# Order of gate products, routing parts, turned inputs and scatters in a gated cross-attention with a mixture of experts

## Chip, core and metric

The kernel runs on one core of a Trainium2 chip. The metric is the device time in microseconds of one execution. A profiled execution adds a trace, from which the views below are taken; its span runs from the first to the last instruction.

## What is computed

All tensors are float32. x is 32 x 112 x 256, the context 32 x 375 x 256.

```python
x = x + tanh(g_xattn) * xattn(ctx, layernorm(x))     # 16 heads of 64
x = x + tanh(g_ffn) * ffn(layernorm(x))

def xattn(ctx, lat):                 # per batch element
    kv = concat([ln_m(ctx), ln_l(lat)])      # 487 keys
    q, (k, v) = ln_l(lat) @ Wq, split(kv @ Wkv)
    return softmax(q @ k.T / 8) @ v @ Wout
def ffn(x):                          # 3584 tokens, 8 experts, the best 2
    s = softmax(x @ gate_w); w, e = top_k(s, 2); w = w / w.sum()
    return sum(w[j] * (gelu(x @ w1[e[j]] + b1[e[j]]) @ w2[e[j]] + b2[e[j]]))
```

## The kernel before

**Attention.** Two batch elements share a group g of eight steps; step n = 8g + m works on four heads of one element, and there are 128 steps (LAST = 128, NG = 4). The engines run in the order in which the Python code issues instructions (a manual schedule): each engine has a queue, and an instruction that waits holds all behind it on its engine. Step n issues, in the loop from L1201: the score matmuls (`scores`, L449) of step n+1, the row maxima on VectorE (L459), the exponentials on ScalarE (L469); then five slots h = 0 to 4. A slot holds products of keys and values on TensorE (lists `slots` and `pe`), then for h < 4 the four transposes of one head's probabilities (`turn_attn`, L490, copied by VectorE at L494, for h = 2 by ScalarE), the division of half the probabilities (`norm`, L481 and L483), small parts left by an earlier slot (`soon_`, on GpSimd), the VectorE parts of the slot (list `dve`), one pending scatter (`outgoing`) and one pending part of the routing (`extra`). At the start of an even step n the output of the two steps before it is formed (`attend`, L504).

**Keys and values.** Each pair of batch elements needs seven products of blocks instead of eight (`seven`). The first and fourth (p1, p5) are copied by ScalarE (L400, L412), p6 and p7 are added to those by VectorE (L404, L408), GpSimd then adds two blocks (L394), and p2, p4, p3 are added by VectorE (L418). In odd steps p1, p6, p7, p5 are of keys and p2, p4, p3 of values; in even steps the other way round. The sums of inputs that these products use are made by GpSimd (`input_sums`, L333) in step m = 4, one per slot.

**PSUM.** All products, transposes and turned inputs share four buffers (tag `m`, pool `ps_m`). As the trace has it, a new tile takes the buffer that was let go first. Scores and expert outputs have two others (`ps_s`).

**Inputs.** A batch element's context and x are normalised (statistics L227 and L228 in m = 6, 7; roots L248 to L257 on GpSimd in the next slot, applied by ScalarE, L261, in m = 0, 2) and turned in m = 1 and m = 3 of the group before their use (`turn`, L291), half k = 0 copied by ScalarE (L299), half k = 1 by VectorE (L303).

**Slabs and gates.** Tokens are handled in 28 slabs of 128; a group g > 0 has up to two finished slabs, u = 0 and u = 1. `project` (L539, m = 0), `residual` (L549 and statistics, with a GpSimd root L559, L561 left in `soon_`), `normed` (L567 on VectorE, then a copy L570 on GpSimd in the next slot) and `logits_of` (a product L577 of 128 x 256 per expert, eight per slab, with a read of 0.08 us) belong to a slab. `normed` and six products are in step m = 2 + 2u, two in each of h = 1 to 3; the last two products come in h = 0 of the step after.

**Routing.** Slabs form routing groups of 4, 4, 4, 4, 4, 4, 2 and 2. In the step of a group's last two products `extra` gets the routing's parts, which are popped one per slot: eight parts of small VectorE and GpSimd work; `counts` (L632 to L635, GpSimd); `places` (two matmuls, L641 of `both` and L642 of `had`, which `counts` makes); `gates` (reads the place tile at L646); for the first group the stranger parts (L698, L710); `slots_of` (L662); `out_to`, which fills `outgoing` with one scatter (L673, an indirect DMA on GpSimd's queue) per slab and choice. Routings begin in steps 27, 45, 61, 83, 99, 117 and 125.

**Towards the experts.** In step 120 `counted` (L752) takes the counts so far, and `locate_early` finds the first six blocks of 128 rows; SP loads them in step 123 (`fetch_rows`, L875) after the scatters issued up to then. `turn_rows(t)` turns the rows of block t (L893) and copies them (L897); `hidden(t)` (L906, L913) and `second(t)` (L919) are the expert's two layers; `combine(t)` scales (L935) and adds into the output by an indirect DMA on GpSimd's queue (L936). Blocks 0 to 2 are begun in steps 125 to 127 and in the tail after the loop, where also the last two slabs are projected, routed on VectorE and scattered, and `locate_late` (L761 to L806) finds the other blocks. Then `run` works through the blocks.

Of the kernel before, what the change touches and what calls it, by code (L numbers as in the profile page):

```python
# [23 lines left out]
def kernel(  # L24
# [20 lines left out]
    nc = tc.nc  # L45

    P = 128
    B, S, D = x.shape
# [38 lines left out]
    NG = NP // 2  # L87
# [78 lines left out]
    if True:  # L166
# [45 lines left out]
        outgoing = []  # L212
# [785 lines left out]
        def do(parts):  # L998
            for part in parts:
                part()  # L1000
# [63 lines left out]
        LAST = B * NG  # L1064
        fills = {1: 3, 2: 3, 3: 2}
        sums_at = {0: (0, 2), 1: (1, 1), 2: (0, 3), 3: (1, 2), 4: (0, 0), 5: (1, 3)}
        filled, extra = 0, []
        for n in range(LAST):
            if n % NG == 0:
                b = n // NG  # L1070
                if b + 4 < B:
                    load(b + 4)
                for _ in range(fills.get(b, 0)):
                    fill(filled)
                    filled += 1
            g, m = divmod(n, 2 * NG)


            jk, jv, odd = (n + 3) // 2, n // 2, n % 2
            for kv, j in ((0, jk), (1, jv)):  # L1080
                if (kv, j) not in ahead and j < LAST // 2:
                    ahead[kv, j], behind[kv, j] = seven(kv, j)
            none = [lambda: None] * 4
            one, two = ((1, jv), (0, jk))[odd], ((0, jk), (1, jv))[odd]
            one, two = ahead.get(one, none), behind.get(two, none)
            if n < LAST - 5:
                slots = [[two[0], one[0]], [two[1]], [one[1], two[2]], [one[2]], [one[3]]]
            else:

                for j in (LAST // 2 - 2, LAST // 2 - 1):  # L1090
                    if (1, j) not in ahead:
                        ahead[1, j], behind[1, j] = seven(1, j)
                (p1, p6, p7, p5), (p2, p4, p3) = ahead[1, LAST // 2 - 2], behind[1, LAST // 2 - 2]
                (q1, q6, q7, q5), (q2, q4, q3) = ahead[1, LAST // 2 - 1], behind[1, LAST // 2 - 1]
                slots = {
                    5: [[two[0], one[0]], [two[1], one[1]], [two[2], p1], [one[2], p6], [one[3]]],
                    4: [[two[0], p7], [two[1], p5], [two[2], p2], [p4, q1], [p3, q6]],
                    3: [[q7], [q5], [q2], [q4], [q3]],
                }.get(LAST - n, [[], [], [], [], []])

            qn = [n] if n < LAST - 8 else {LAST - 8: [n, n + 1], LAST - 7: [n + 1, n + 2, n + 3]}.get(n, [])
            for n_ in qn:
                qg, qi = divmod((n_ + 3) // 2, NG)
                if qg < B // 2:
                    slots[1].insert(0, lambda qg=qg, i=qi + NG * (1 - n_ % 2): q_unit(qg, i))

            pe = [[], [], [], [], []]
            dve = [[], [], [], []]  # L1110
            if n in sums_at:
                dve[1].append(lambda: weight_sums(*sums_at[n]))

            nb = 2 * g + 2
            if nb < B:
                if m in (0, 2):
                    for h in range(4):
                        dve[min(h + 1, 3)].append(then[nb + m // 2][h])
                if m == 1:
                    pe[1] += [lambda: turn(nb, 0), lambda: turn(nb, 1, nc.vector)]  # L1120
                if m == 3:
                    pe[1] += [lambda: turn(nb + 1, 0), lambda: turn(nb + 1, 1, nc.vector)]
                if m == 4:
                    for h, part in enumerate(input_sums(g + 1)):
                        dve[h].append(part)
                if m in (6, 7) and nb + 2 < B or n == 1:
                    u = m - 4 if m > 1 else 1
                    ln_now, then[nb + u] = ln_parts(nb + u)
                    for h in range(4):
                        dve[h].append(ln_now[h])  # L1130
            if n == 1:
                nc.scalar.activation(tg[:, :2], tg[:, :2], AF.Tanh)
                nc.scalar.mul(tg[:, 2:3], tg[:, 1:2], 0.5)
            if n == 3:
                dve[2].append(b1_turned)

            for u in range(2):
                i = ended(2 * g - 2 + u) if g > 0 else None
                if m == 6 + u and ended(2 * g + u) is not None:
                    load_slab(ended(2 * g + u))  # L1140
                if i is None:
                    continue
                if m == 0:
                    pe[2 + 2 * u].append(lambda i=i: project(i))
                if m == u:
                    dve[3 - 3 * u].append(lambda i=i: residual(i))
                if m == 2 + 2 * u:
                    dve[0].append(lambda i=i: normed(i))
                    for h in range(1, 4):
                        dve[h].append(lambda h=h, i=i: logits_of(i, 2 * h - 2, 2 * h))  # L1150
                if m == 3 + 2 * u:
                    dve[0].append(lambda i=i: logits_of(i, 6, 8))
                    if group[i][1] == groups[group[i][0]] - 1:

                        r, (hits, ids, ids_out) = route_parts(group[i][0], nc.gpsimd)
                        extra = [[part] for part in r[:11]]
                        if group[i][0] == 0:

                            at = [(j, e) for j in range(2) for e in range(0, E, 2)]
                            for k in range(len(at) + 1):  # L1160
                                extra.append([lambda p=p: ids(*p) for p in at[k - 1 : k] if k > 0])
                                extra[-1] += [lambda p=p: hits(*p) for p in at[k : k + 1]]
                            extra.append([ids_out])
                        extra += [[part] for part in r[11:]]

            if n == LAST - 8:
                pe[0].append(lambda: found.update(ps=counted()))
                early = locate_early()
                dve[1].append(lambda: next(early))
            if n == LAST - 7:  # L1170
                for h in range(3):
                    dve[h].append(lambda: next(early))
            if n == LAST - 6:
                soon.close()
                weight_buffers(ctx.enter_context(tc.tile_pool(name="wexp", bufs=1, side="right")), 0)
                found["early"] = ctx.enter_context(tc.tile_pool(name="early", bufs=1, side="right"))
                fetch_weights(0)
            if n == LAST - 5:
                for t in range(NE):
                    fetch_rows(t)  # L1180
            if n == LAST - 3:
                pe[4].append(lambda: turn_rows(0))
            if n == LAST - 2:

                pe[0].append(lambda: others(ends))
                pe[1] += [lambda: hidden(0, 0, 3)]
                pe[2] += [lambda: hidden(0, 3, 5)]
                pe[3].append(lambda: hidden(0, 5, 7))
                pe[4] += [lambda: hidden(0, 7, 8), lambda: turn_rows(1, nc.scalar.copy)]
            if n == LAST - 1:  # L1190
                for h in range(4):
                    pe[h].append(lambda h=h: hidden(1, 2 * h, 2 * h + 2))
                pe[4].append(lambda: turn_rows(2, nc.scalar.copy))

            if n > 0 and n % 2 == 0:
                attend(n // 2 - 1)
            more = n + 1 < LAST
            if more:
                scores(n + 1)
                exps(n + 1, 0)  # L1200
            for h in range(5):  # L1201
                for unit in slots[h] + pe[h]:
                    unit()
                if h == 4:
                    break
                turn_attn(n, h)
                if more and h in (1, 3):
                    norm(n + 1, h // 2)
                then_ = soon_[:]
                del soon_[:]  # L1210
                do(then_)
                for part in dve[h]:
                    part()
                if outgoing:
                    outgoing.pop(0)()
                if extra:
                    do(extra.pop(0))
                if more and h == 0:
                    exps(n + 1, 1)
# [38 lines left out]
        found["ps"] = counted()  # L1258
        do(r[10:])
        do(outgoing)  # L1260
        locate_late()
        combine(0)
        combine(1)
        for t in range(NE, NE + AHEAD):
            fetch_rows(t)
        hidden(3)
        turn_rows(4)
        combine(2)


# [57 lines left out]
```

## Time and profile before

| what | us |
|---|---|
| median of 3 runs | 2166.86 (2163.98 to 2167.33) |
| the profiled execution | 2170.11 |
| its span | 2168.3 |
| TensorE busy | 2121.5 |
| VectorE busy | 1267.6 |
| ScalarE busy | 1203.6 |
| GpSimd busy | 711.4 |
| mean granted TensorE clock | 0.994 |

A line of a view names the engine (PE is TensorE, PEld its weight loads, DVE VectorE, ACT ScalarE, POOL GpSimd, SP the queue that issues most DMAs), the line of the kernel, the operation and out<-in tiles. Timeline lines begin with the start and the duration in us; a bracket has the idle time of the engine before it and what ended that. In tables by stage each engine has its busy time, with the number of instructions in parentheses, and the last three numbers are the share of full TensorE clock, the busy share of the DMA engines and GB/s. Steps 1 to 127 of the loop fill the stretch from 38.9 us to 1719.8 us; the tail follows.

### The profile page before, as it was taken

The numbers are of one execution on the slowest core, as the hardware profiler recorded it, in microseconds if no ns is written. First come the engines' busy times: TensorE is split into PE (matmuls) and PEld (weight loads), VectorE is DVE, ScalarE is ACT, GpSimd is POOL, SyncE is SP. The second block draws the span as 40 slices with busy tenths as digits, with TensorE's granted clock in tenths as the row PEclk, the third lists the DMA queues.
The fourth block names the chain that finished last, engine by engine and source line by source line (L and its number), as shares of the span: only waits on it lengthen the run. The fifth ranks groups of instructions, "written<-read, shape, count | busy, mean of one in ns | idle before, by whom it ended". The sixth has DMA issues, their size and how long they took to land. (4 is left out here: it accounts for less than half of the span.)

```text
span 2168.3 us, 41569 instructions
## 1 busy us (share of the span) xinstructions
PE 2121.5 (98%) x15944; PEld 1664.4 (77%) x15944; DVE 1267.6 (58%) x2782; ACT 1203.6 (56%) x2889; POOL 711.4 (33%) x992
## 2 busy tenths in 40 slices
PE   9999999999999999999999999999999899999998
PEld 5777777777767776777777777777777789999997
DVE  5667676767676767576767676757677431111111
ACT  5666565556655665566665656566655434343433
POOL 5422332443233323332325332433233222222222
PEclk9999999999999999999999999999999999999999
DMA  6692000010001000100000000000002346655553
GB/s 147 202 330 70 17 13 18 13 39 8 16 13 37 13 18 13 39 8 15 13 18 25 25 13 27 16 20 4 10 7 79 101 128 188 175 163 160 144 138 67
DMA packets 113696, 138.17 MB, mean 64 GB/s; under 512 B 14704, under 2 KB 101432, under 8 KB 113368
## 3 DMA queue, kind: packets, MB, share of 16 engines
q1 hardware_dynamic: 101032, 119.11, 17.8%
q0 software_dynamic: 11328, 15.33, 3.9%
q8 instruction: 127, 2.08, 0.4%
q10 hardware_dynamic: 1136, 1.05, 0.2%
q14 instruction: 73, 0.60, 0.1%
HBM read 166.84 MB, written 48.99 MB: 100 GB/s over the span
## 5 line engine op out<-in xcount | busy, mean ns | idle before, releaser
L483 ACT ACTIVATE ex<-ex,rc 112x487 f32<-112x487 f32 x512 | 331.0, 694 | 360.8 <-DVE rc L481 358.9
L459 DVE TENSOR_REDUCE nmx<-ps_s 112x2 f32<-112x974 f32 x256 | 288.0, 1166 | 322.5 <-PE ps_s L449 322.3
L469 ACT ACTIVATE ex<-ps_s,nmx 112x487 f32<-112x487 f32 x512 | 337.3, 667 | 155.8 <-DVE nmx L459 154.2
L490 PEld LDWEIGHTS ps_t<-ident,ex 112*122 112x122 f32 x2048 | 233.0, 139 | 141.2 <-issue 94.9
L913 ACT ACTIVATE h<-ps_h,b 128x128 f32<-128x128 f32 x480 | 175.6, 367 | 259.0 <-PE ps_h L906 210.9
L490 PE MATMUL ps_t<-ident,ex 112*122 112x112 f32 x2048 | 283.8, 261 | 17.3 <-DVE tmpv L404 13.1
L494 DVE COPY exT<-ps_t 122x448 f32<-122x448 f32 x384 | 236.9, 617 | 38.4 <-PE ps_t L490 38.4
L449 PE MATMUL ps_s<-kT,qT 64*112 64x487 f32 x1024 | 242.0, 591 | 0.0
L394 POOL TENSOR_TENSOR vv<-tmpv,vv 122x512 f32<-122x512 f32 x64 | 81.3, 1270 | 467.4 <-ACT vv L412 447.3
L906 PE MATMUL ps_h<-xsT,w 128*128 128x128 f32 x1920 | 228.7, 277 | 6.1 <-issue 2.6
L906 PEld LDWEIGHTS ps_h<-xsT,w 128*128 128x128 f32 x1920 | 226.7, 194 | 9.9 <-issue 2.8
L504 PEld LDWEIGHTS ps_o<-exT,vv 122*64 122x64 f32 (+1 forms) x4096 | 197.6, 136 | 44.7 <-issue 31.0
L919 PE MATMUL ps_y<-w,h 128*128 128x256 f32 x960 | 216.8, 379 | 0.0
L504 PE MATMUL ps_o<-exT,vv 122*64 122x112 f32 (+1 forms) x4096 | 211.3, 260 | 0.0
L384 PE MATMUL ps_v<-wkv_s,tT 128*122 128x128 f32 x1536 | 201.5, 274 | 0.0
L936 POOL DMA_INDIRECT out_dram<-y,xs x60 | 93.4, 1557 | 313.0 <-DVE y L935 173.4
L919 PEld LDWEIGHTS ps_y<-w,h 128*128 128x128 f32 x960 | 178.0, 190 | 21.8
L378 PE MATMUL ps_k<-tT,wkv_s 128*128 128x487 f32 x378 | 192.4, 592 | 0.0
L384 PEld LDWEIGHTS ps_v<-wkv_s,tT 128*122 128x122 f32 x1536 | 181.9, 185 | 2.2 <-issue 1.8
L384 PEld LDWEIGHTS ps_v<-wkv,kvT 128*122 128x122 f32 x1024 | 125.8, 185 | 74.2 <-issue 58.8
L394 POOL TENSOR_TENSOR kT<-tmpk,kT 128x487 f32<-128x487 f32 x63 | 77.0, 1222 | 305.4 <-ACT kT L412 305.2
L418 DVE TENSOR_TENSOR kT<-ps_k,kT 128x487 f32<-128x487 f32 x189 | 124.5, 659 | 50.3 <-PE ps_k L378 43.7
(215 smaller groups left out, 3154.5 us busy)
## 6 DMA issues: line engine op xcount, KB each, us to landing
w<-in_L_ffn_w_dram SPq DMA_DIRECT2D x120, 1024.0 KB
xg<-pad SPq DMA_DIRECT2D x8, 3640.0 KB
cin<-in_ctx_dram SPq DMA_DIRECT2D x32, 336.0 KB
xs<-xg SPq DMA_DIRECT2D x60, 130.0 KB
b<-in_L_ffn_b_dram SPq DMA_DIRECT2D x60, 128.0 KB
xin<-in_x_dram SPq DMA_DIRECT2D x32, 112.0 KB
x<-in_x_dram SPq DMA_DIRECT2D x28, 128.0 KB
out_dram<-x SPq DMA_DIRECT2D x28, 128.0 KB
```

The lines of the kernel that those rows point to most:

```text
L378: nc.tensor.matmul(ps, lhsT=w[:, 0, i * P : (i + 1) * P], rhs=x[:, :NK], start=True, stop=True)
L384: nc.tensor.matmul(ps[:, c, :], lhsT=x[:, c * KC : (c + 1) * KC], rhs=w[:, 1, i * P : (i + 1) * P], start=True, stop=True,)
L449: nc.tensor.matmul(ps[:, j, :NK], lhsT=qT[b // 2, i][r, b % 2, :], rhs=kT[b, i][r, :], start=True, stop=True,)
L459: nc.vector.tensor_reduce(nmx[b, i], pss[b, i][:, :, :NK], AX.X, ALU.max, negate=True)
L469: nc.scalar.activation(t[:, j, :NK], ps[:, j, :NK], AF.Exp, bias=nmx[b, i][:, j : j + 1], accum_out=sm[b, i][:, j : j + 1],)
L483: nc.scalar.mul(ex[b, i][:, j, :NK], ex[b, i][:, j, :NK], rc[:, j : j + 1])
L490: nc.tensor.transpose(ps[:, c, :], ex[b, i][:, j, c * KC : (c + 1) * KC], ident[:S, :S])
L494: (nc.scalar.copy if h == 2 else nc.vector.tensor_copy)(exT[b, i, j], ps)
L504: nc.tensor.matmul(ps[y * DH : (y + 1) * DH, r, x * S : (x + 1) * S], lhsT=vv[j][:m, c, x, r, y * DH : (y + 1) * DH], rhs=exT[2 * g + x, i ...
L906: nc.tensor.matmul(ps, lhsT=w1t[:, k, f * P : (f + 1) * P], rhs=xsT[t][:, k, :], start=(k == 0), stop=(k == KD - 1),)
L913: nc.scalar.activation(hid[t][:, f, :], ps, AF.Gelu, bias=b1t[:, f : f + 1])
L919: nc.tensor.matmul(psy[t], lhsT=hid[t][:, f, :], rhs=w2t[:, f, :], start=(f == 0), stop=(f == NF - 1),)
```

## The change

- `normed` and `logits_of` of slab u = 1 move from m = 4 and 5 to m = 5 and 6, except in the last group (nb >= B). Routings that follow a slab u = 1 begin a step later: 46, 62 and 118 instead of 45, 61 and 117.
- `extra` gets an empty slot between `counts` and `places`.
- The turn of half k = 1 in m = 1 and m = 3 moves from slot 1 to slot 2, behind that slot's products.
- Scatters are popped in slots h = 0 and h = 2 only, until step 124; after that in every slot, as before.
- The rows of blocks 1 and 2 are copied by VectorE instead of ScalarE.
- `turn_rows(4)` is issued ahead of `locate_late`, the first two `combine` and `hidden(3)` instead of behind them.

```diff
                 if m == 1:
-                    pe[1] += [lambda: turn(nb, 0), lambda: turn(nb, 1, nc.vector)]
+                    pe[1].append(lambda: turn(nb, 0))
+                    pe[2].append(lambda: turn(nb, 1, nc.vector))
                 if m == 3:
-                    pe[1] += [lambda: turn(nb + 1, 0), lambda: turn(nb + 1, 1, nc.vector)]
+                    pe[1].append(lambda: turn(nb + 1, 0))
+                    pe[2].append(lambda: turn(nb + 1, 1, nc.vector))
...
-                if m == 2 + 2 * u:
+                m_ = 2 + 2 * u if nb >= B else 2 + 3 * u
+                if m == m_:
                     dve[0].append(lambda i=i: normed(i))
                     for h in range(1, 4):
                         dve[h].append(lambda h=h, i=i: logits_of(i, 2 * h - 2, 2 * h))
-                if m == 3 + 2 * u:
+                if m == m_ + 1:
                     dve[0].append(lambda i=i: logits_of(i, 6, 8))
                     if group[i][1] == groups[group[i][0]] - 1:
                         r, (hits, ids, ids_out) = route_parts(group[i][0], nc.gpsimd)
-                        extra = [[part] for part in r[:11]]
+                        extra = [[part] for part in r[:9]] + [[]] + [[part] for part in r[9:11]]
...
-                pe[4] += [lambda: hidden(0, 7, 8), lambda: turn_rows(1, nc.scalar.copy)]
+                pe[4] += [lambda: hidden(0, 7, 8), lambda: turn_rows(1)]
...
-                pe[4].append(lambda: turn_rows(2, nc.scalar.copy))
+                pe[4].append(lambda: turn_rows(2))
...
-                if outgoing:
+                if outgoing and (h % 2 == 0 or n > LAST - NG):
                     outgoing.pop(0)()
...
         do(outgoing)
+        turn_rows(4)
         locate_late()
         combine(0)
         combine(1)
         for t in range(NE, NE + AHEAD):
             fetch_rows(t)
         hidden(3)
-        turn_rows(4)
         combine(2)
```

## Prediction

> **What bounds the kernel.** I read the page first: TensorE is busy nearly throughout and its clock is all but full, so only TensorE's idle stretches and its slow stretches can be won. The page's TensorE row, then the waits of TensorE alone (total, times, longest):
>
> ```profile
> PE 2121.5 (98%) x15944; PEld 1664.4 (77%) x15944; DVE 1267.6 (58%) x2782; ACT 1203.6 (56%) x2889; POOL 711.4 (33%) x992
> ```
> ```profile
> PE ps_t L490 <- DVE tmpv L404: 13.1, 11, 1.2
> PE ps_pos L642 <- POOL had L634: 6.8, 5, 2.6
> PE ps_v L384 <- DVE vv L418: 3.0, 4, 0.8
> PE ps_t L490 <- ACT qT L317: 2.9, 10, 0.3
> PE ps_h L906 <- issue: 2.6, 1, 2.6
> PE ps_h L906 <- POOL macc L635: 2.0, 1, 2.0
> PE ps_t L490 <- DVE kT L418: 1.1, 1, 1.1
> ```
>
> I then cut the span where each step n begins (its first score matmul, L449, which is for step n+1) and compared steps of one kind. Columns: stretch, length, busy TensorE, weight loads, VectorE, ScalarE, GpSimd, then the granted clock. In order: n=4, 20 (both m=4), 21 (m=5), 22 (m=6), 23 (m=7), 29 (m=5 with a routing), 47 (m=7 with a routing), 104.
>
> ```profile
> 78.47:88.78 10.31, 10.31 (x68) 7.58 (x66) 7.23 (x12) 5.85 (x15) 7.71 (x10) 1.00 1.09 335
> 284.90:296.62 11.72, 10.53 (x69) 7.60 (x67) 9.56 (x19) 5.91 (x16) 6.53 (x6) 1.00 0.17 56
> 296.62:310.17 13.55, 13.55 (x125) 9.94 (x125) 9.92 (x23) 8.63 (x19) 3.77 (x3) 1.00 0.00 1
> 310.17:320.48 10.31, 10.31 (x68) 7.57 (x66) 8.35 (x17) 5.91 (x16) 1.23 (x2) 1.00 0.00 0
> 320.48:333.97 13.49, 13.49 (x125) 10.02 (x124) 9.88 (x24) 8.73 (x19) 6.21 (x11) 1.00 0.00 1
> 401.36:417.24 15.88, 14.53 (x130) 10.50 (x129) 11.87 (x31) 8.84 (x20) 7.41 (x16) 1.00 0.00 1
> 639.19:658.89 19.70, 17.08 (x129) 12.52 (x128) 10.52 (x26) 8.94 (x20) 9.13 (x24) 0.83 0.00 0
> 1405.08:1420.50 15.42, 14.33 (x85) 10.48 (x83) 7.17 (x12) 9.48 (x22) 8.70 (x15) 1.00 0.10 36
> ```
>
> A clean even step takes 10.31 us, a clean odd one 13.49. Step 4 holds the input sums but no gate products and is clean; step 20 has both and is 1.41 longer. The timeline there shows why: a gate product (L577, 0.42 us in step 18) takes 1.23 while GpSimd adds (L333); L404 comes late, and the transpose needs the PSUM tile that L404 reads.
>
> ```profile
> 291.66 1.23 POOL L333 TENSOR_TENSOR tT<-kvT 128x488 f32<-128x488 f32 x1
> 291.94 1.23 DVE L577 CUSTOM_DVE_ANT_0 junk<-xr,gw_sb 128x256 f32<-128x256 f32 x1
> 294.46 0.68 DVE L404 TENSOR_TENSOR tmpv<-ps_v,vv 122x512 f32<-122x512 f32 x1
> ```
>
> The routing's place matmul (L642) waits 2.6 us for GpSimd's counts in steps 47 and 63, and afterwards the same key product takes 1.97 us for 1.00: the clock is halved.
>
> ```profile
> 648.15 0.64 PE L642 MATMUL ps_pos<-had,ones 128*128 128x32 f32 x2 [2.62 <-POOL had L634]
> 648.60 1.97 PE L378 MATMUL ps_k<-tT,wkv_s 128*128 128x487 f32 x2
> ```
>
> At the end two copies are late:
>
> ```profile
> 1711.76 0.36 ACT L897 COPY xsT<-ps_x 128x256 f32<-128x256 f32 x1
> 1750.99 0.42 DVE L897 COPY xsT<-ps_x 128x256 f32<-128x256 f32 x1
> ```
>
> TensorE starts 0.1 us after the first (L906 at 1712.21, put down to POOL, which was long done) and 0.1 after the second (1751.52).
>
> **What the skill says.** The Trainium skill, "SBUF — State Buffer", Who interferes with whom: a VectorE instruction with two SBUF inputs contends with a GpSimd one that reads SBUF, and the loser blocks fully. The trace agrees (1.23 beside L333, 0.42 alone). "TensorE: Matmul & The Clock Gate", What's actually happening: the clock goes to half after an idle window of about 3.4 us, and windows run freely. Here the half clock lasts (1-0.83) x 2 x 19.70 = 6.7 us in step 47, two such windows, but 2.6 us of idling were enough; 1.2 us (step 20, clock 1.00) were not.
>
> **The change, part by part** (against the profiled run: 2170.1 us, span 2168.3 and 1.8 around it; it lies 3.2 above the median of 2166.9).
>
> *Gate products of the second slab from m=4/5 to m=5/6.* One L567 (0.41), eight L577 (0.50 with its read) and GpSimd's copy L570 (0.40) move. Out of m=4: eleven steps (12, 20, 36, 44, 52, 60, 68, 76, 92, 108, 116) fall from 11.72 to 10.31: 11 x 1.41 = **-15.5**. Into m=5: VectorE has 9.9 busy of 13.55, less 1.0 of old products and 1.0 of products spilled from m=4, plus 3.4: 11.3, which fits; GpSimd's value adds (L394) end 4.6 us into the step (n=5), ahead of the products in h=1. Into m=6: 8.35+1.0 of 10.31 fits too. Tightest is the tile that L418 frees for the last product of the step, with 0.1 us of slack; I take 0.05 a step, 14 steps, **+0.7**; both ends 0 and 0.5. Without that cover it is 1.2 a step. SP: the slab load L528 waits for L567 (290.07 after 290.04) and so goes a step (12 us) later, with the input loads behind it; those are wanted by statistics over 100 us later: nothing.
>
> *A slot between counts and places.* A slot is about 2.6 us of TensorE work (two products and a transpose: 1.0+1.05+0.55). For routings of a second slab (steps 47 and 63) the counts also slip to h=0 of the next m=0, where GpSimd finishes them some 5.5 us into a step in which places are wanted at 13. Away go 19.70-13.49 and 19.90-13.49 (step 63): 12.6. Back come the matmuls (0.45 each, from step 119: 13.94-13.49) and, I estimate, 0.35 because the place tile occupies one of four PSUM buffers over h=3, and 0.3 in step m=6 for the routing parts: 2.2 for both. **-10.4.** Steps 29, 85, 101 (15.87 each): 2.3 over clean; matmuls 0.45 stay and about 0.6 comes back, since the attention outputs then wait for h=3's L408 instead of ScalarE's copy: 3 x 1.3 = **-3.9** (ends 2 and 5.5). The stranger parts slip a slot too, and meet two products in step 30: **+0.5**.
>
> *Scatters in even slots.* Step 104 (15.42 for 13.77 in step 40) stalls since a scatter in each slot waits for the one before (starts 2.7 to 2.9 us apart) and GpSimd's key adds queue behind: **-1.65**. Eight scatters last four steps instead of two; in m=4 two of 1.0 us meet 6.5 to 7.7 of other GpSimd work in 10.31: fits, no reader waits there. Near the end five scatters of group 5 now come after the row loads on SP (issued 1656.38 to 1660.86) and wait for them on GpSimd's queue, value adds and the next slab's copy behind them; also group 5's counts come after the early count in step 120. I put **+0.5** there (0 to 2).
>
> *Turned inputs in two slots.* In m=3 the transpose waits for qT's copy. With the second turn in h=2, k6 inherits that buffer and waits for the same copy; the work between is the same. **-0.5** (0 to 5.9, all that m=3 loses, which I exclude since ScalarE's copy does not move).
>
> *Two copies from ScalarE to VectorE, one turn earlier.* In step 126 VectorE is free at 1710.34 and the transposes end at 1710.22: copy to 1710.8, so L906 starts 1.3 earlier, and matmuls at the half clock there save 0.8: -2.1. But places now come at h=2 of step 127, so the tail's scatters start 0.8 later against TensorE, the chain over L561, normed, products and routing with them: TensorE is 1.3 early when that chain releases it. Turning block 4 ahead of L779 to L806 removes the 2.58 gap; L761 behind the copy costs 0.4 back. Block 3's y waits for a POOL scatter (VectorE free only at 1762.88), which caps the gain there. Together **-3.3** (1 to 5).
>
> Sum: -15.5 +0.7 -10.4 -3.9 +0.5 -1.65 +0.5 -0.5 -3.3 = -33.6. 2170.1-33.6 = 2136.5 for a profiled run; from the median, 2166.9-33.6, about **2133**.
>
> **Rivals.** *Given back in m=6:* an even step has no slack, and routing and statistics are there already. For it: step 124, with products beside value adds, loses 0.94. Against: step 18 carries 3.4 us of products in 10.31 without loss. 14 x 1.2 = 17 more: 2150. *The counts are still late*, since GpSimd does roots in m=0 too, or the slot does not move the release: B's 10.4+3.9 stay: 2147. *Slower: contention goes with the products.* If value adds in m=5 ran beside h=1 to h=3, each of six products would take 1.3 for 0.42: 5.3 against 2.2 of slack, 3.1 a step; over some 2 us idle in a window the clock halves and adds 3.1: 14 x 6.2 = 87, less 34: 2220. It decides from the point where the adds start 3 us later than now (ScalarE's copy L412 gates them); nothing in m=5 delays that copy.
>
> **Numbers.** Forecast 0.76, giveback 0.12, late counts 0.08, contention 0.04. The first alone spans 2126 to 2141 from the ends above; reaching to the rivals gives 2126 to 2149. Faster by over 0.2% (4.3 us, about what a measurement can tell from no change) in all but the last: 0.95; same 0.015, slower 0.035.
>
> **What would show it.** Right: no wait of L490 for L404 left; m=4 at 10.31 throughout; no half clock before 1650 us; L642 without waits; step 104 at 13.8. Wrong: m=5 or m=6 over 14.0 or 10.8, L577 at 1.3 us in m=5, GpSimd idle before L673 for DMAs of xs, or the gap before block 4 still there.

## The result and the profile after

The changed kernel takes 2140.38 us (median of 4, 2139.07 to 2141.24), the kernel before beside it 2166.56: a ratio of 0.9881 (95% interval 0.9864 to 0.9898), 26.2 us less. Forecast were 2133 and a gain of 33.6. The profiled execution of after took 2140.79, span 2139.1; before's was 2168.3. The page's TensorE row, then the longest waits of TensorE (total, times, longest):

```profile
PE 2111.2 (99%) x15944; PEld 1660.0 (78%) x15944; DVE 1249.4 (58%) x2784; ACT 1206.4 (56%) x2887; POOL 708.5 (33%) x992
```
```profile
PE ps_x L893 <- DMA xs<-xg: 5.2, 1, 5.2
PE ps_k L378 <- ACT qT L317: 3.3, 10, 0.3
```

The 13.1 us of L490 waiting for L404 and the 6.8 of L642 waiting for GpSimd's counts are gone. The 2.9 of L490 waiting for qT have become 3.3 of L378 waiting for the same copy. On top stands a wait that the kernel before doesn't have: 5.2 us for rows (xs). The table by step of after, in order n=20, 21, 29, 47, 48 (columns as above; clock third from the end):

```profile
285.00:295.31 10.31, 10.31 (x68) 7.57 (x66) 7.14 (x12) 5.91 (x16) 6.00 (x6) 1.00 0.01 3
295.31:308.81 13.50, 13.50 (x125) 10.02 (x125) 9.88 (x27) 8.73 (x19) 3.41 (x4) 1.00 0.15 48
...
399.83:413.92 14.09, 14.09 (x129) 10.54 (x128) 10.32 (x31) 8.84 (x20) 6.74 (x15) 1.00 0.16 46
...
633.77:647.26 13.49, 13.49 (x125) 10.01 (x124) 10.71 (x30) 8.59 (x19) 7.18 (x16) 1.00 0.00 0
647.26:665.58 18.32, 17.92 (x104) 13.98 (x102) 8.44 (x16) 9.85 (x24) 7.51 (x22) 1.00 0.03 8
```

Step 20 fell from 11.72 to 10.31, step 29 from 15.88 to 14.09, step 47 from 19.70 to 13.49 with a full clock; step 48 rose from 17.22 to 18.32, where the places now are. At the end the sign turns. The next two tables hold, for before and then for after, the stretch from the last routing's place matmul (L642) to the turn of block 6 (L893), and that turn with what follows up to hidden(6):

```profile
1744.43:1762.41 17.98, 15.39 (x122) 14.78 (x121) 6.91 (x41) 8.32 (x23) 5.67 (x5) 1.00 0.19 49
1762.41:1766.08 3.67, 3.67 (x20) 3.26 (x19) 1.11 (x3) 0.49 (x2) 1.70 (x1) 1.00 0.46 100
```
```profile
1710.42:1731.27 20.85, 15.54 (x121) 14.78 (x121) 7.10 (x41) 8.81 (x24) 5.61 (x5) 0.93 0.48 149
1731.27:1736.93 5.66, 5.66 (x19) 4.69 (x20) 1.11 (x3) 0.00 (x0) 1.69 (x1) 0.65 0.42 83
```

TensorE works 15.4 and 15.5 us in the first stretch, but it takes 2.9 longer, and the second takes 2.0 longer at a clock of 0.65. In the first stretch after's DMA moves 149 GB/s, before's 49. The timelines say what moves. First the first two of before's last four scatters, then after's weight load, its first two scatters, the row loads and TensorE (start, duration, idle before and its end in brackets):

```profile
1746.92 1.10 POOL L673 DMA_INDIRECT xg<-xr,sloti  x1 [10.58 <-issue]
1750.90 1.02 POOL L673 DMA_INDIRECT xg<-xr,sloti  x1 [2.88 <-DMA xg<-xr,sloti]
```
```profile
1711.12 0.39 SPq L888 DMA_DIRECT2D w<-in_L_ffn_w_dram  x1
...
1712.92 1.11 POOL L673 DMA_INDIRECT xg<-xr,sloti  x1 [10.59 <-issue]
1719.60 0.96 POOL L673 DMA_INDIRECT xg<-xr,sloti  x1 [5.58 <-DMA xg<-xr,sloti]
...
1728.48 2.96 SPq L875 DMA_DIRECT2D xs<-xg  x4
...
1731.27 0.66 PE L893 MATMUL ps_x<-ident,xs 128*128 128x128 f32 x2 [5.25 <-DMA xs<-xg]
```

A scatter waits for the one before it. The second starts 4.0 us after the first in before and 6.7 in after, where 2.2 MB of weights of block 5 are under way at the same time (from 1710.5 to 1727 the hardware queue moved 2.23 MB; in before, from 1744.5 to 1758, none). The rows of block 6 are loaded behind the last scatter, and TensorE stands before them.

By the steps of the prediction, in the profiled executions:

| term | predicted | measured |
|---|---|---|
| eleven steps m=4 | -15.5 | -15.5 |
| tightness in m=5, m=6 | +0.7 | -0.6 |
| counts, steps 46 to 48, 62 to 64 | -10.4 | -10.2 |
| steps 29, 85, 101 | -3.9 | -5.3 |
| steps 30, 32 | +0.5 | +0.7 |
| step 104 | -1.65 | -1.65 |
| steps 118 to 125 | +0.5 | +0.7 |
| turned inputs | -0.5 | -0.1 |
| step 126 to the last places, then to the end | -3.3 | -3.4, +4.8 |
| start-up to step 1 | none | +1.4 |
| sum | -33.6 | -29.2 (as the spans have it) |

The 1.4 at the start are no part of the change's effect: step 1 begins between 38.8 and 40.5 us in the runs below, in kernels of both kinds.

### The profile page after: what moved, and what is told of

Its sections match the earlier page's. It is cut to its first block, busy times and chain, and to the rows that moved or that the text cites. A ratio compares the mean times of both kernels' runs of the same rounds, so it can differ in the third digit from the quotient of the medians.

```text
span 2139.1 us, 41500 instructions
## 1 busy us (share of the span) xinstructions
PE 2111.2 (99%) x15944; PEld 1660.0 (78%) x15944; DVE 1249.4 (58%) x2784; ACT 1206.4 (56%) x2887; POOL 708.5 (33%) x992
## 2 busy tenths in 40 slices
DMA packets 116896, 142.63 MB, mean 67 GB/s; under 512 B 15088, under 2 KB 104120, under 8 KB 116568
## 5 line engine op out<-in xcount | busy, mean ns | idle before, releaser
L483 ACT ACTIVATE ex<-ex,rc 112x487 f32<-112x487 f32 x512 | 331.1, 694 | 328.2 <-DVE rc L481 323.3
L459 DVE TENSOR_REDUCE nmx<-ps_s 112x2 f32<-112x974 f32 x256 | 288.0, 1167 | 312.7 <-PE ps_s L449 311.7
L490 PEld LDWEIGHTS ps_t<-ident,ex 112*122 112x122 f32 x2048 | 231.8, 138 | 118.3 <-issue 96.9
L490 PE MATMUL ps_t<-ident,ex 112*122 112x112 f32 x2048 | 280.8, 259 | 0.2 <-DVE exT L494 0.2
L494 DVE COPY exT<-ps_t 122x448 f32<-122x448 f32 x384 | 237.4, 618 | 37.8 <-PE ps_t L490 36.6
L906 PEld LDWEIGHTS ps_h<-xsT,w 128*128 128x128 f32 x1920 | 224.2, 192 | 6.7 <-ACT h L913 1.8
L906 PE MATMUL ps_h<-xsT,w 128*128 128x128 f32 x1920 | 226.3, 275 | 2.7 <-ACT h L913 1.2
L919 PE MATMUL ps_y<-w,h 128*128 128x256 f32 x960 | 218.6, 381 | 0.0
L384 PE MATMUL ps_v<-wkv_s,tT 128*122 128x128 f32 x1536 | 202.0, 274 | 1.2 <-DVE vv L408 1.2
L919 PEld LDWEIGHTS ps_y<-w,h 128*128 128x128 f32 x960 | 179.3, 192 | 22.4
L378 PE MATMUL ps_k<-tT,wkv_s 128*128 128x487 f32 x378 | 189.4, 583 | 3.4 <-ACT qT L317 3.3
L384 PEld LDWEIGHTS ps_v<-wkv_s,tT 128*122 128x122 f32 x1536 | 181.9, 185 | 4.0 <-issue 1.8
L384 PEld LDWEIGHTS ps_v<-wkv,kvT 128*122 128x122 f32 x1024 | 125.9, 185 | 74.3 <-issue 56.7
L418 DVE TENSOR_TENSOR kT<-ps_k,kT 128x487 f32<-128x487 f32 x189 | 124.7, 660 | 47.7 <-PE ps_k L378 42.6
```

The source lines that it names most:

```text
L378: nc.tensor.matmul(ps, lhsT=w[:, 0, i * P : (i + 1) * P], rhs=x[:, :NK], start=True, stop=True)
L384: nc.tensor.matmul(ps[:, c, :], lhsT=x[:, c * KC : (c + 1) * KC], rhs=w[:, 1, i * P : (i + 1) * P], start=True, stop=True,)
L459: nc.vector.tensor_reduce(nmx[b, i], pss[b, i][:, :, :NK], AX.X, ALU.max, negate=True)
L483: nc.scalar.mul(ex[b, i][:, j, :NK], ex[b, i][:, j, :NK], rc[:, j : j + 1])
L490: nc.tensor.transpose(ps[:, c, :], ex[b, i][:, j, c * KC : (c + 1) * KC], ident[:S, :S])
L494: (nc.scalar.copy if h == 2 else nc.vector.tensor_copy)(exT[b, i, j], ps)
```

## The experiments

All times are medians. The runs are in three sets, each on another chip: block4_back to gates_alone, slot_back to after_again, and the other four. The kernel before took 2164.05, 2164.61 and 2165.51 beside them, and the ratio of each run is to the one of its set. A difference of two kernels under some 2 us is read from the traces; each trace is of one execution.

| run | us | ratio (95%) |
|---|---|---|
| block4_back | 2139.32 | 0.9878 (0.9862 to 0.9895) |
| second_first | 2138.27 | 0.9874 (0.9857 to 0.9890) |
| group5_early | 2137.78 | 0.9873 (0.9857 to 0.9890) |
| gates_alone | 2147.32 | 0.9919 (0.9904 to 0.9934) |
| slot_back | 2139.55 | 0.9883 (0.9867 to 0.9899) |
| slot_alone | 2157.20 | 0.9967 (0.9956 to 0.9978) |
| scatters_back | 2145.67 | 0.9916 (0.9901 to 0.9930) |
| after_again | 2141.33 | 0.9891 (0.9876 to 0.9907) |
| turns_back | 2140.86 | 0.9872 (0.9856 to 0.9889) |
| copies_back | 2141.66 | 0.9876 (0.9859 to 0.9892) |
| sums_on_vector | 2164.47 | 0.9991 (0.9983 to 0.9998) |
| better | 2132.31 | 0.9836 (0.9822 to 0.9851) |

**block4_back**: what the earlier turn of block 4 is worth.

```diff
         do(outgoing)
-        turn_rows(4)
         locate_late()
...
         hidden(3)
+        turn_rows(4)
         combine(2)
```

> The kernel after with turn_rows(4) put back behind hidden(3); nothing else. Theory (block 6's rows come when the last group's four scatters are through, whatever TensorE does): the 2.58 us gap before block 4 returns, the gap before block 6 falls from 5.2 to about 2.7, and the time stays within 2 us of the kernel after (2138 to 2142). Rival (the copy of block 4's rows on VectorE stands ahead of the locating of the late blocks and so holds up the row loads): rows land earlier, 2137 or less. The prediction's own sum (the earlier turn is worth what it removes): 2142.5 or more.

2139.32. TensorE waits 2.58 us before block 4 and 2.50 before block 6, where after waits 5.25 at once. The earlier turn only carries TensorE sooner to rows that come when they come: it is worth nothing, and the copy doesn't hold up the locating.

**second_first**: is TensorE only standing there?

```diff
             for t in range(begin, end):
                 hidden(t)
-                if t + 1 < end:
-                    turn_rows(t + 1)
-                if t > begin or follow:
+                if follow and t == NE - 1:
                     second(t - 1)
                     combine(t - 1)
+                    turn_rows(t + 1)
+                    second(t)
+                    combine(t)
+                else:
+                    if t + 1 < end:
+                        turn_rows(t + 1)
+                    if (t > begin or follow) and not (follow and t == NE):
+                        second(t - 1)
+                        combine(t - 1)
```

> The kernel after with the second layers of blocks 4 and 5 around the turn of block 6: hidden(5), second(4), turn_rows(6), second(5), hidden(6), instead of hidden(5), turn_rows(6), second(4), hidden(6), turn_rows(7), second(5). Theory (TensorE only stands before block 6's rows, which land at a time of their own): 3.6 us of second(4) fill the gap, which falls from 5.2 to about 1.6, the half clock behind it (1.8 us) goes, 2135. Rival (the end is set by the chain of combines on GpSimd or by the loads of weights): no change, 2140.

2138.27, less of a gain than forecast. The gap before block 6 falls to 1.48, but three new ones follow: 0.83 (L919 behind VectorE's L929, the sum that makes y, which has three buffers and so stands behind a combine), 1.54 (L906 behind the copy of block 6's rows, which VectorE does after that sum) and 0.60. So the rival was partly right: the chain of combines is next in line, through VectorE's queue.

**group5_early**: where the weights come from. The early count stands ahead of group 5's counts in step 120, since that routing now begins in step 118. With 20 slabs counted in place of 24, block 5 can fall to another expert; a block after the third has its weights loaded only when it needs another expert than the block three before it. This kernel puts group 5's routing back to step 117, and pops a scatter in every slot from step 120 on.

```diff
-                m_ = 2 + 2 * u if nb >= B else 2 + 3 * u
+                m_ = 2 + 2 * u if nb >= B - 2 else 2 + 3 * u
...
-                if outgoing and (h % 2 == 0 or n > LAST - NG):
+                if outgoing and (h % 2 == 0 or n > LAST - 9):
```

> The kernel after with the gate products of group 5's last slab back in m=4 and 5 (its routing begins in step 117 again, and its counts come before the early count of step 120), and from step 120 on a scatter in every slot. Theory (leaving group 5 out of the early count makes block 5 another expert than block 2, so its weights are really fetched, 2 MB, and the last scatters stand behind them): no weights between 1711 and 1714 us, last scatters about 2.8 to 4 us apart instead of up to 6.7, the gap before block 6 about 2.4 instead of 5.2 and no half clock: 4.6 less; back come 1.4 for step 116 and 0.5 to 1 for scatters: 2137.5. Rival (TensorE has only come earlier to rows that were always so late after the last routing): the gap stays over 4 us, 2142.

2137.78, as forecast. The bytes of the whole execution fall from 142.63 to 138.17 MB, before's figure; the last four scatters start 3.3, 2.7 and 2.9 us apart; the gap before block 6 is 1.8 us, and the clock stays full. So of the 5.2 us some 3.5 come of the weights, and the rest of TensorE's being early. gates_alone, which slips the same routing, moves 142.63 MB too, and slot_alone, which doesn't, 138.17. In the ten traces of this document with the load the second of the last four scatters starts 6.7 to 7.8 us after the first, in the four without it 3.3 to 4.0. The 4.46 MB are two loads of weights; the second lies between 1728 and 1788 us in after (10.40 MB of the hardware queue, for 8.16 in the same stretch of before) and delays nothing, since from hidden(6) to the end both kernels take 402.2 us.

**gates_alone**: the kernel before with the moved products and nothing else.

```diff
-                if m == 2 + 2 * u:
+                m_ = 2 + 2 * u if nb >= B else 2 + 3 * u
+                if m == m_:
...
-                if m == 3 + 2 * u:
+                if m == m_ + 1:
```

> The kernel before with the move of the second slab's gate products alone. By the prediction's term the eleven steps m=4 fall from 11.72 to 10.31, 15.5 in all; m=5 and m=6 stay at 13.5 and 10.3. The routings of two of the groups slip a step with it, so their counts come in h=0 and their places in h=1 of an m=0 step. If the slip does not help, the waits for the counts stay and it gives 2151; if the slip alone takes the counts out of the way, a further 6 to 12 go and it gives 2139 to 2145. If the contention only moves with the products: 2166 or more.

2147.32 lies between 2151 and the 2139 to 2145, and the trace holds the surprise. Steps 29, 47 and 48 of it:

```profile
398.72:412.81 14.09, 14.09 (x129) 10.50 (x129) 10.69 (x32) 8.95 (x20) 6.35 (x15) 1.00 0.15 46
632.27:645.76 13.49, 13.49 (x125) 10.02 (x124) 10.71 (x30) 8.60 (x19) 7.19 (x16) 1.00 0.00 1
645.76:663.43 17.67, 17.67 (x104) 13.95 (x102) 8.46 (x16) 9.85 (x24) 7.32 (x24) 1.00 0.03 8
```

Without any empty slot steps 29 and 47 are as short as in after, and step 48, with the places in it, shorter (17.67 to 18.32). From step 1 to step 126 this kernel takes 1631.1 us, after 1627.9 and before 1659.8: the moved products bring 28.8 of the 32.0. In steps 47 and 63 the slip does it, by the trace, as no run slips a routing alone: in before L634 stands behind value adds and roots and starts 8.2 us into step 47 (647.34 less 639.19), while TensorE waits; now it starts 5.1 us into step 48 (650.84 less 645.76), and TensorE comes to the places at 6.0 (651.74) without a wait. Step 29 has no slip. In before TensorE waits twice in it, and the counts are the shorter wait:

```profile
407.27 1.14 PE L384 MATMUL ps_v<-wkv,tT 128*122 128x128 f32 x8 [0.84 <-DVE vv L418]
409.46 0.41 PE L642 MATMUL ps_pos<-had,ones 128*128 128x32 f32 x2 [0.51 <-POOL had L634]
```

The timelines of ScalarE and GpSimd tell why both waits go, before first, then gates_alone:

```profile
403.59 1.29 ACT L483 ACTIVATE ex<-ex,rc 112x487 f32<-112x487 f32 x2 [3.66 <-DVE rc L481]
404.53 0.25 POOL L627 TENSOR_TENSOR both<-s,s 128x32 f32<-128x32 f32 x1 [2.23 <-DVE s L623]
405.43 1.26 POOL L394 TENSOR_TENSOR vv<-tmpv,vv 122x512 f32<-122x512 f32 x1 [0.64 <-ACT vv L412]
...
408.45 0.96 POOL L634 TENSOR_TENSOR had<-had,both 128x8 f32<-128x8 f32 x3
```
```profile
398.89 1.29 ACT L483 ACTIVATE ex<-ex,rc 112x487 f32<-112x487 f32 x2 [1.60 <-DVE rc L481]
399.02 0.25 POOL L627 TENSOR_TENSOR both<-s,s 128x32 f32<-128x32 f32 x1 [0.53 <-DVE s L623]
400.73 1.27 POOL L394 TENSOR_TENSOR vv<-tmpv,vv 122x512 f32<-122x512 f32 x1 [1.45 <-ACT vv L412]
...
403.57 0.91 POOL L634 TENSOR_TENSOR had<-had,both 128x8 f32<-128x8 f32 x3
```

In before, VectorE works on six gate products of the other slab, two of them slowed by GpSimd's sums. Four stand ahead of its reciprocal L481 and two more ahead of L623, L459 and L418, so all of these are late. ScalarE's L483 waits for L481. Behind L483 on ScalarE's queue stands L412, the copy for which the value adds wait in both timelines: it starts 3.4 us into the step (404.79 less 401.36) against 1.4 (400.09 less 398.72). Behind the adds come the counts: L634 7.1 us into the step (408.45 less 401.36) against 4.9 (403.57 less 398.72). So the products held up both waits, and I had priced the counts alone. What is lost against after lies in steps 123 (17.24 for 14.48, with a wait of 2.40, see scatters_back) and 104 (15.23 for 13.77). The other executions of gates_alone lie 5 to 7 us above its profiled one (2142.2), at a mean clock of 0.996 or 0.997 for its 0.999.

**slot_back** and **slot_alone**: the empty slot taken from after, and put alone into before.

```diff
-                        extra = [[part] for part in r[:9]] + [[]] + [[part] for part in r[9:11]]
+                        extra = [[part] for part in r[:11]]
```

> The kernel after without the empty slot between counts and places; the rest as it is. The prediction's term: the waits for the counts come back in steps 29, 47, 63, 85, 101 and with them the half clock, 14.3 us more: about 2154. The theory formed on the run with the gate products alone: moving those products alone already brings the counts in time (VectorE no longer holds the routing's parts behind products, and two routings slip into a step in which GpSimd is free), so the empty slot is worth nothing or a little less: steps 48 and 64 fall from 18.3 to 17.7, 32 from 17.7 to 17.2, 120 from 19.3 to 18.8: 2.2 less, 2138.

2139.55, against 2141.33 of after on the same chip. Steps 29 and 47 stay at 14.09 and 13.49; 48 and 64 fall to 17.67, 32 to 17.22, 120 to 18.84; 86 and 102 rise by 0.28. Forecast by the prediction's term were 2154. On top of the other edits the slot costs 1.5 us from step 1 to step 126.

> The kernel before with the empty slot alone. If the slot is a remedy of its own for the same wait (the prediction's term, without the slip): steps 47 and 63 fall from 19.8 to about 13.5 to 14.5 and the half clock there goes, steps 29, 85, 101 fall from 15.9 to about 14.1 to 14.6, m=4 stays at 11.7: 2150 to 2154. If only the products on VectorE held the counts up: 29, 85, 101 stay near 15.9 and the whole is 2158 or more.

2157.20: between the two. Its steps 29 and 47:

```profile
401.27:416.43 15.16, 14.32 (x130) 10.42 (x129) 11.38 (x30) 8.73 (x20) 7.39 (x16) 1.00 0.00 1
638.37:653.01 14.64, 14.12 (x129) 10.54 (x128) 10.32 (x26) 8.84 (x20) 8.66 (x22) 1.00 0.00 1
```

Alone it brings step 47 from 19.70 to 14.64, since half a microsecond of wait is left and the clock stays full, but step 29 only from 15.88 to 15.16: there the 0.51 us for L634 are gone and the 0.84 for L418 stay. So it is a second remedy for a wait that the moved products take away too, and the weaker one.

**scatters_back**: a scatter in every slot.

```diff
-                if outgoing and (h % 2 == 0 or n > LAST - NG):
+                if outgoing:
```

> The kernel after with a scatter in every slot again. The prediction's terms: step 104 goes back to 15.4, 1.65 more, and the 0.5 at the end comes back: 2141.5. Theory after the run with the gate products alone: since group 5's routing has slipped a step, its scatters reach into step 123 and hold the value adds on GpSimd there: 2.4 more at TensorE in step 123 beside 1.5 in step 104 and 0.5 in 86, 88 and 102, and the clock at half for a window behind it in most executions: 2144 to 2148.

2145.67, 4.3 over after_again. Steps 88 and 104 get 0.7 each, and step 123 gets 2.6: there L384 waits 2.24 us for L418. GpSimd and then VectorE in that step:

```profile
1633.22 0.96 POOL L673 DMA_INDIRECT xg<-xr,sloti  x1 [1.72 <-DVE vv L418]
1634.21 1.27 POOL L394 TENSOR_TENSOR vv<-tmpv,vv 122x512 f32<-122x512 f32 x1
```
```profile
1633.59 2.19 DVE L577 CUSTOM_DVE_ANT_0 junk<-xr,gw_sb 128x256 f32<-128x256 f32 x1
```

The scatters hold the value adds up: they begin 5.7 us into step 123 (1634.21 less 1628.47), against 2.6 in after (1630.04 less 1627.36). The next L418 changes a block that the second add reads, and so waits for its end (1636.89; L418 starts at 1637.11). The gate products in between take 2.19 and 1.36 us for 0.42, as in the rival "contention goes with the products", but they aren't the cause: in gates_alone they take 0.42 in step 123, and VectorE waits all the same:

```profile
1635.53 0.69 DVE L418 TENSOR_TENSOR vv<-ps_v,vv 122x512 f32<-122x512 f32 x1 [3.09 <-POOL vv L394]
```

So the even slots are worth more than I gave them (1.65, with a cost of 0.5 at the end), because the moved products, with which group 5's routing slips a step, make them needed in step 123. In step 104 they bring only 0.7 of the 1.65: without them it takes 14.44, with gates_alone 15.23, so the rest comes of the other edits together.

**after_again**: the kernel after, to set these against.

> The kernel after itself, unchanged, on the same chip as the three others, to set them against: 2138 to 2141.

2141.33; the gap before block 6 is 5.15. One of the six executions took 5588.39 us, for a reason that no trace shows; the others lie between 2140.39 and 2141.86.

**turns_back**: both turns in slot 1.

```diff
-                    pe[1].append(lambda: turn(nb + 1, 0))
-                    pe[2].append(lambda: turn(nb + 1, 1, nc.vector))
+                    pe[1] += [lambda: turn(nb + 1, 0), lambda: turn(nb + 1, 1, nc.vector)]
```

(and the same for m = 1)

> The kernel after with both turns of m=1 and of m=3 in slot 1 again. The prediction's term: 0.5 less with the split, so 0.5 more here. Theory from the traces of before and after: the wait for ScalarE's copy of qT only goes from the transposes (0.29) to the key product (0.33), so m=3 stays at 14.9 and the time within 0.5 us of the kernel after: 2140.5 to 2142.

2140.86: no difference. Steps 27, 83 and 99 take 15.08 for 14.91; the other seven 14.86 for 14.91; step 1 14.51 for 14.64.

**copies_back**: the rows of blocks 1 and 2 by ScalarE.

```diff
-                pe[4] += [lambda: hidden(0, 7, 8), lambda: turn_rows(1)]
+                pe[4] += [lambda: hidden(0, 7, 8), lambda: turn_rows(1, nc.scalar.copy)]
```

(and the same for block 2)

> The kernel after with the rows of blocks 1 and 2 copied by ScalarE again. The prediction's term: TensorE starts block 1 1.3 us later (the gap is 2.0 instead of 0.75). Theory: the gap comes back, but the time changes by less than that, 0 to 0.6, since TensorE later waits 5.2 us for block 6's rows all the same; those rows hang on the last slabs' routing, which comes up to 1.2 later: 2141.5 to 2142.5. The prediction's full term (with the half clock): 2143.4.

2141.66. The gap before block 1 is 1.99 again (0.72 to 0.75 with VectorE), but the one before block 6 did not shrink, it is 5.8. By the trace the last places come 1.2 us later in the stretch from step 126 than in the first run of after (43.44 for 42.22), as the prediction had it; in after_again, where 3.4 us of half clock fall there, they come as late (43.51); the times (0.3 over after_again, 1.3 over the first run of after) are too close to say how much of that reaches the end.

**sums_on_vector**: is it the contention that made m=4 long?

```diff
-                lambda o=o, l=l, r=r: nc.gpsimd.tensor_tensor(o, l, r, ALU.subtract)
+                lambda o=o, l=l, r=r: nc.vector.tensor_tensor(o, l, r, ALU.subtract)
```

> The kernel before with the input sums (L333) made by VectorE instead of GpSimd; the gate products stay in m=4 and 5. Theory (a gate product, with two SBUF inputs, takes 1.2 to 1.3 us for 0.42 because GpSimd reads SBUF beside it): the products run at 0.42 again, and although VectorE gets four more additions of some 0.6 us, the eleven steps m=4 fall from 11.72 to 10.3 to 10.6: 12 to 15 less than the kernel before, about 2150. Rival (VectorE simply has too much ahead of L404 in m=4): with 2.4 us more on VectorE the steps stay at 11.7 or get longer: 2165 or more.

2164.47: nothing gained, although half of the theory holds. Steps 20 and 21 of it:

```profile
285.29:295.62 10.33, 10.33 (x68) 7.59 (x66) 8.78 (x18) 5.92 (x16) 1.61 (x2) 1.00 0.20 62
295.62:310.57 14.95, 13.77 (x126) 9.94 (x125) 11.11 (x28) 8.63 (x19) 3.76 (x3) 1.00 0.01 2
```

With no sums on GpSimd the products take 0.42 us, L404 is in time and m=4 is clean at 10.33, which settles the contention. But VectorE, with 0.65 us for each sum, is behind by the end of the step, and m=5 stalls instead (14.95; L384 waits 1.19 us for L418). Where the products leave m=4, as in after, both steps are clean.

**better**: the kernel after without the empty slot, with another order at block 6 and five buffers for y.

```diff
-            ys[t] = found["tiles"].tile([P, D], F32, tag="y", name=f"y_{t}", bufs=3)
+            ys[t] = found["tiles"].tile([P, D], F32, tag="y", name=f"y_{t}", bufs=5)
...
-                        extra = [[part] for part in r[:9]] + [[]] + [[part] for part in r[9:11]]
+                        extra = [[part] for part in r[:11]]
...
+                if follow and t == NE - 1:
                     second(t - 1)
                     combine(t - 1)
+                    second(t)
+                    turn_rows(t + 1)
+                    combine(t)
```

(the rest as in second_first)

> The kernel after without the empty slot, with the order hidden(5), second(4), second(5), turn_rows(6), hidden(6) at block 6, and with five buffers for y instead of three, so that VectorE's sums of the second layers no longer wait for combines. Theory: the 6.3 us gap before block 6 of the run without the slot is filled with 7.2 us of second layers, of which about 0.8 (the copy of block 6's rows) stays open, and the half clock behind it goes: 5.5 + 1.7 less than 2139.6: about 2132.5. Rival (the chain of combines on GpSimd or the loads of weights set the end once TensorE is earlier): 2136 or more, with new waits after block 6.

2132.31, 9.0 below after_again, by three edits together; the slot's share is some 1.5 to 1.8 (slot_back). TensorE at block 6 in it:

```profile
1722.82 7.07 PE L919 MATMUL ps_y<-w,h 128*128 128x256 f32 x32
...
1730.63 3.84 PE L906 MATMUL ps_h<-xsT,w 128*128 128x128 f32 x32 [0.52 <-DVE xsT L897]
```

The second layers of blocks 4 and 5 fill the time in which the rows come, and the clock stays full. The weights still slow the scatters (the second starts 7.3 us after the first), but nobody waits for it.

## Why the prediction was right, and where not

**Right:** m=4 (-15.5 of -15.5), and the size of the whole of steps 1 to 126: predicted -30.3 without the tail, measured -32.0. The work moved into m=5 and m=6 found room, since value adds and products don't meet there: every product of m=5 takes 0.40 to 0.43 us in after. The sum of 11.3 us for VectorE in m=5 was too high (9.88 in step 21), as it left out that a sum and a copy of m=4 had spilled there with the products (L408 at 296.44 and L494 at 297.04, 0.69 and 0.61 us, in before); so m=5 became 0.05 us shorter and not longer. The Trainium skill's "SBUF — State Buffer" (Who interferes with whom), by which a VectorE instruction with two SBUF inputs contends with a GpSimd one that reads SBUF, holds here: the slowdown to 1.23 us goes when GpSimd's sums go (sums_on_vector).

**Right in size, wrong in cause:** "A slot between counts and places", -10.4 and -3.9. gates_alone has these gains without the slot, slot_back keeps them without it. The step that failed is that I asked what the slot moves and not what holds TensorE and the counts up: in step 29 VectorE's products, in 47 by the trace the step in which the counts come. Step 104 is of this kind too: its -1.65 came, but the even slots account for 0.7 of it (scatters_back).

**Failed:** "Two copies ... one turn earlier", "Together -3.3". The 1.3 at block 1 and the 2.58 before block 4 went as said. But the next late thing was named as block 3's y, and it was block 6's rows: they hang on the last places, four scatters in a row and the loads behind them, whatever TensorE does. In before TensorE came to them without a wait; after came 2.4 us earlier against the last places (15.60 us behind L642, which is the stretch of 20.85 less the wait of 5.25, for 17.98), and the four scatters took 3.0 us longer (from the first start to the last, 13.1 for 10.1). Measured for this part: +1.4 instead of -3.3, and +3.0 in after_again, which has 3.4 us of half clock in step 126 (472.55 from step 126 to the end, before 469.54). I had seen that group 5's counts come after the early count and put 0 to 2 us on it, without asking what the early blocks are then: block 5 no longer has block 2's expert, so its weights are loaded, and that load meets the last scatters. group5_early and block4_back show the two halves.

**Base:** the sum was taken from one profiled execution and subtracted from the median. Before's profiled execution holds more half clock than most (its mean clock is 0.994, that of the 24 executions of the last set 0.993 to 0.999, only two of them as low): 3.3 us in step 47 ((1-0.83) x 19.70), 3.4 in 63 (0.83 over 19.90), 3.2 after step 126 (0.93 over 45.65). It lies 3.2 above the median, which is about the difference between the 29.3 that the profiled executions gained (2170.11 to 2140.79) and the 26.2 of the medians. Each sum belongs to its own execution.

No rival came in the kernel after: m=6 has 0.1 us more in two routing steps, m=5 stays at 13.50 without a routing. One of the signs of being wrong came, without a cost: in step 123 GpSimd is idle for 1.58 us before L673 (1634.25) for a DMA of xs, and the step takes 14.48 us for 14.49. What spreads the start over 1.7 us, and how much of the copies' 1.2 us reaches the end, stays open.

## What to carry to other kernels

When two edits aim at one wait, ask what each would do alone: here a product moved away from a slowed engine removed the wait that a spacer was meant for, and the spacer then cost time. A stall taken from the busiest engine is gained only up to the next thing that comes at a time of its own; follow such a chain (routing, scatters, row loads) to its end before pricing it, and put work that needs nothing of it in front. And ask what an edit does to the data that decide later work: here a routing that came a step too late for a count changed which weights are loaded.

## What was not expected of the hardware

An indirect scatter of 128 rows lands in time for the next to start 2.7 to 4.0 us after it when no weights are loaded beside it (group5_early, before), and only after 6.7 to 7.8 us when 2.2 MB of weights are under way. Idle stretches alike were followed by different clocks: 2.6 us came with 6.8 us of half clock (step 47 in before), 2.58 with 3.4 us of it and 2.50 with none (block4_back), and 2.58 before block 4 in before with none. So the prediction's "some 2 us idle in a window" is no threshold that these runs bear out. "TensorE: Matmul & The Clock Gate" in the Trainium skill (What's actually happening) says that windows run freely, which fits.
